# A four-layer kernel on one core: a twelfth paged sequence, staggered attention tiles, layer input added by VectorE, a later gate, and a new written order

## The chip, the cores and the metric

The kernel runs on one core of a Trainium2 chip. Its engines are PE (TensorE, matrix products), DVE (VectorE), ACT (ScalarE), POOL (GpSimd, here mostly the issuer of indirect DMAs) and SP (which issues the plain DMAs). Each engine takes its instructions in the order of the program; semaphores hold an instruction back until what it needs is there. The metric is the device time of one execution in microseconds (us), as the median of several runs.

## The reference, cut to what matters

The input is 8 sequences of 512 tokens with 128 features. Four layers follow, each added to its input, which is normalised first:

```
x = x + attention(layernorm(x))      # one head, causal, softmax
x = x + ffn(layernorm(x))            # 32 experts, 4 per token, and a shared expert
x = x + rwkv(layernorm(x))           # time mixing with a scan over the tokens, then channel mixing
x = x + ffn(layernorm(x))            # the same weights again
```

The expert layer, `swiglu(x, w1, w2, w3) = silu(x @ w1) * (x @ w3) @ w2`:

```
scores = softmax(x @ Wg); weights, indices = top_k(scores, 4)
for e in range(32):
    tok = tokens that chose e, the first C = 2048 of them
    y[tok] += swiglu(x[tok], W1[e], W2[e], W3[e]) * weight
y += swiglu(x, Ws1, Ws3, Ws2)        # the shared expert, for every token
```

W1 and W3 are 128 x 64 per expert, W2 is 64 x 128. Everything is in float32.

## The kernel before, in words

**Where things lie.** The 8 sequences stay on the chip in `res[b]` (128 tokens x 4 blocks x 128 features) through all four layers; all weights are loaded once. Matrix products write into PSUM tiles: `light` gives one of four single banks, and `ps2` has two tiles of two banks for the wide results.

**Streams.** The work is cut into streams, Python generators that are advanced one step at a time: `a0` to `a7` (`attention`, which ends in the routing `route` of the first expert layer), `r0` to `r7` (`rwkv`, ending in the routing of the second expert layer), and for the two expert layers (first letter small or other for the first, the next for the second) `x`/`y` (`shared`), `s`/`t` (`scatter`), `u`/`v` (`combine`), `d`/`D` (`full_up`), `e`/`E` (`full_down`) and the four stages of a group of experts `k l m n`/`K L M N` (`turned`, `up`, `down`, `give`, L558 to L617). The string `ORDER` (L82), two letters a step, is the order written out by hand in which these steps are issued; `play` walks it. Since all engines keep the program's order, this string decides what stands ahead of what on every engine, the DMA queues of SP and POOL included.

**The expert layers, two ways.** `RUNS` (L35) says for each of the two expert layers which sequences are done how.

- *Full* (`full_up`, `full_down`): every token of the sequence goes through all 32 experts, two at a time (16 pairs). PE makes two products of 128 x 512 per pair (L706), ACT the tanh (L709), DVE three passes (L712 to L714), the last two with the gates, which come back from DRAM by broadcasting loads (L695). `full_down` sums all pairs in one PSUM tile: it starts with the identity times the layer's input (L722), then adds four products per pair (`down_on`, L676), and ACT copies the sum into `res` (L727).
- *Paged*: `route` gives every (token, choice) a row in a buffer in DRAM in which rows of one expert fill whole pages of 128. `scatter` (L505) writes the normalised rows there: 16 indirect DMAs per sequence from POOL, a short memset after each (`pause`, L307). A group of sequences shares the pages: a group of three has 80 pages, a group of two 64, taken in units of four. Per unit, `turned` loads the pages and transposes them (L345, copy L563), `up` multiplies by the expert's weights (L575), DVE computes the gate's exponent (L580), ACT the tanh and the exponential (L583, L584), and DVE makes the gated product (L586, L587) and multiplies it by the gate (L588, L589). `down` transposes it (L596, copies L601), and `give` multiplies by the second weights (L608), copies the result (L614) and stores it in DRAM on SP's queue. `combine` (L656) then adds the results into `res`: 16 indirect DMAs with addition per sequence from POOL. The first of them needs all units of the group.

In the first expert layer, sequences 1 to 3 and 4 to 6 are paged groups and 0 and 7 are full; in the second, 0 to 2 and 4 to 5 are groups and 3, 6 and 7 are full: 11 paged, 5 full. Sequences of the second layer use the same two DRAM buffers again. Group (f, g) below is group g of expert layer f, both counted from 0.

**The shared expert** (`shared`, L519): two products with the normalised input, tanh and two DVE passes between, then the identity times the layer's input (L537) and four products with Ws2 into one PSUM tile, which ACT copies into `res` (L540).

**Attention** (`attention`, L732): after the norm and the three projections, four query tiles of 128 are done one after the other, each in seven steps: scores (L762), mask and row maximum, the maximum times minus the scale (L767), exponential with row sum (L771), transposes (L775) and a copy, product with V (L782), and the sum into `res` (L787).

## Time and profile before

| | |
|---|---|
| median of three runs | 837.41 us (836.06 to 840.99) |
| the profiled execution | 835.56 us, span 833.9 us |
| granted TensorE clock, mean | 0.977 |
| PE busy | 766.4 us (92%) |
| DVE busy | 607.6 us (73%) |
| POOL busy | 569.7 us (68%) |
| ACT busy | 472.0 us (57%) |
| indirect DMAs issued by POOL | 176 scatters, 176 gathers |

The span runs from the first to the last instruction of one profiled execution. Busy time is the union of an engine's instructions; what an engine spends on issuing a DMA's descriptors counts, the short gap before each issue does not. The page gives the span in 40 slices of 20.8 us, a digit per slice in tenths of busy time, and the granted TensorE clock in the same way. Groups of instructions are given by line: engine, operation, what is written and read, the count, the busy time, the mean length of one in ns, and the engine's idle time just before them with what ended it. A table by stage has for each stretch its length and then PE's, the weight loads', DVE's, ACT's and POOL's busy time with the number of instructions, the granted clock, the DMA engines' share and GB/s. In lists of waits a line has the waiting instruction, what released it, and the total us, times and longest us.

### The profile page before, as it was taken

The page shows a single profiled execution, that of the slowest core. Times are in us where ns is not written, and L with a number is a line of the kernel's source. Part 1 is how long each engine was busy: PE and PEld are TensorE (multiplying, and loading weights), DVE is VectorE, ACT ScalarE, POOL GpSimd, SP SyncE. Part 2 cuts the span into 40 slices and gives each one's busy share as a digit, 9 for nine tenths or more (in the row PEclk, how much of TensorE's full clock was granted, in tenths as well). Part 3 has the DMA queues.
Part 4 walks back from the last instruction along what each step waited for, and adds up shares of the span by engine and source line. Part 5 has one row for each costly group of instructions (what it writes and reads, how often), then busy time and mean ns, then how long its engine had stood idle before and what let it go on. Part 6 is the DMA issues. An engine that isn't in the chain of part 4 may idle for free.

```text
span 833.9 us, 14386 instructions
## 1 busy us (share of the span) xinstructions
PE 766.4 (92%) x4206; PEld 536.3 (64%) x4206; DVE 607.6 (73%) x2017; ACT 472.0 (57%) x1124; POOL 569.7 (68%) x634
## 2 busy tenths in 40 slices
PE   3998989899999999897998899999999999999993
PEld 2666667577876686684544555555878986776562
DVE  4677877778777558898867778978898664576672
ACT  3875633445776766673747267354677876542221
POOL 6312888742881887888888888885037057888876
PEclk9999999999999999999999789999999999999997
DMA  9999513533749767455222225253246679777663
GB/s 280 262 200 257 143 44 96 141 90 87 196 127 236 134 137 145 131 111 125 30 29 29 35 27 126 65 131 89 65 116 179 167 175 226 150 149 148 135 124 55
DMA packets 154460, 108.19 MB, mean 130 GB/s; under 512 B 17648, under 2 KB 140912, under 8 KB 154128
## 3 DMA queue, kind: packets, MB, share of 16 engines
q1 hardware_dynamic: 122976, 82.74, 41.0%
q0 software_dynamic: 30976, 23.27, 16.1%
q10 hardware_dynamic: 432, 1.27, 0.5%
q8 instruction: 36, 0.59, 0.3%
q14 instruction: 40, 0.33, 0.2%
HBM read 62.40 MB, written 44.84 MB: 129 GB/s over the span
## 4 chain that ended last, share of the span: by engine, by line
PE 35%; POOL 28%; issue 15%; DVE 10%; DMA 6%; ACT 4%; POOLq 1%; SPq 0%; DVEq 0%; ACTq 0%
POOL res L656 18%; POOL xs L505 6%; PE acl L575 5%; PE ac L706 4%; PE o L608 4%; PE turn_x L345 2%; DMA res<-ys,rows 2%; PE fsum L676 2%; POOL idle L307 2%; PE kv L938 2%; PE kk L929 2%; PE o L782 1%; PE acl L596 1%; PE lg L373 1%; DMA res<-in_x_dram 1%
## 5 line engine op out<-in xcount | busy, mean ns | idle before, releaser
L656 POOL DMA_INDIRECT res<-ys,rows x176 | 282.1, 1603 | 82.7 <-issue 48.4
L505 POOL DMA_INDIRECT xs<-xn,rows x176 | 182.1, 1034 | 79.0 <-issue 27.5
L706 PE MATMUL ac<-fT,pair 128*128 128x512 f32 x320 | 152.1, 599 | 0.0
L709 ACT ACTIVATE fh<-ac 128x512 f32<-128x512 f32 x80 | 47.7, 597 | 101.5 <-PE ac L706 101.0
L676 PEld LDWEIGHTS fsum<-w2s,fh 128*128 128x128 f32 x640 | 79.5, 193 | 23.7 <-DVE fh L714 10.9
L676 PE MATMUL fsum<-w2s,fh 128*128 128x128 f32 x640 | 84.1, 277 | 3.5 <-DVE fh L714 2.8
L706 PEld LDWEIGHTS ac<-fT,pair 128*128 128x128 f32 x320 | 56.5, 193 | 47.4 <-issue 45.9
L575 PE MATMUL acl<-w13s,xgTs 128*128 x608 | 83.0, 280 | 2.2 <-ACT hz L601 0.8
L575 PEld LDWEIGHTS acl<-w13s,xgTs 128*128 128x128 f32 x608 | 75.6, 193 | 13.4 <-issue 5.3
L712 DVE SCALAR_TENSOR_TENSOR fh<-fh,ac 128x512 f32<-128x512 f32 x80 | 54.4, 680 | 40.4 <-ACT fh L709 40.0
L608 PE MATMUL o<-w2s,hz 128*128 x608 | 79.3, 276 | 1.5 <-ACT gT L492 1.3
L608 PEld LDWEIGHTS o<-w2s,hz 128*128 128x128 f32 x608 | 73.9, 192 | 5.6 <-issue 2.6
L601 ACT COPY hz<-acl 64x256 f32<-64x256 f32 x152 | 55.6, 366 | 16.5 <-PE acl L596 14.5
L583 ACT ACTIVATE h<-acl 128x256 f32<-128x256 f32 x76 | 29.1, 382 | 53.6 <-DVE wt L580 50.3
L714 DVE TENSOR_TENSOR fh<-fh,g 128x512 f32<-128x512 f32 x80 | 55.4, 693 | 2.8
L713 DVE TENSOR_TENSOR g<-g,ac 128x512 f32<-128x512 f32 x80 | 54.3, 679 | 0.0
L334 POOL TENSOR_TENSOR rstd_f<-rstd_f,nhalf 128x4 f32<-128x4 f32 x16 | 19.4, 1213 | 49.3 <-DVE wt L580 23.2
L586 DVE SCALAR_TENSOR_TENSOR h<-h,acl 128x256 f32<-128x256 f32 x76 | 31.7, 418 | 25.6 <-ACT h L583 25.4
L307 POOL MEMSET idle<- 128x192 f32 x176 | 49.2, 280 | 0.1
L563 ACT COPY xgTs<-turn_x 128x512 f32<-128x512 f32 x76 | 44.3, 584 | 6.7 <-PE turn_x L345 4.9
L614 ACT COPY oc<-o 128x512 f32<-128x512 f32 x76 | 44.2, 586 | 5.7 <-PE o L608 3.2
L345 PE MATMUL turn_x<-ident,xg 128*128 128x128 f32 x304 | 45.3, 273 | 2.1 <-DMA xg<-xs 2.0
(265 smaller groups left out, 1551.6 us busy)
## 6 DMA issues: line engine op xcount, KB each, us to landing
g<-gd SPq DMA_DIRECT2D x40, 512.0 KB, 6.9
xg<-xs SPq DMA_DIRECT2D x76, 260.0 KB, 3.7
ys<-oc SPq DMA_DIRECT2D x76, 256.0 KB, 2.5
xs<-zero SPq DMA_DIRECT2D x4, 2600.0 KB, 14.6
xs<-xn,rows POOLq DMA_INDIRECT x176
res<-ys,rows POOLq DMA_INDIRECT x176
res<-in_x_dram SPq DMA_DIRECT2D x8, 256.0 KB, 4.5
pair<-in_w_dram SPq DMA_DIRECT2D x1, 2048.0 KB
```

What stands on the lines that cost most here:

```text
L307: nc.gpsimd.memset(idle, 0.0)
L345: nc.tensor.transpose(p[:, j * P : (j + 1) * P], src[:, j, :P], ident)
L505: i = nc.gpsimd.indirect_dma_start(out=xs[g][:, :], out_offset=bass.IndirectOffsetOnAxis(ap=rows[:, j, k : k + 1], axis=0), in_=xn[:, j, : ...
L575: nc.tensor.matmul(acl[:, j, :EW], xT[:, j * P : (j + 1) * P], w13f[:, bass.ds(at[j], EW)], start=True, stop=True)
L601: nc.scalar.copy(z[half, i, :].rearrange("p (j c) -> p j c", c=H), hT[half])
L608: nc.tensor.matmul(o[:, j * P : (j + 1) * P], z[:, j % 2, j // 2 * P : (j // 2 + 1) * P], w2h[j % 2][:, bass.ds(at[j], P)], start=True, st ...
L656: nc.gpsimd.indirect_dma_start(out=xa[:, j, :], out_offset=None, in_=ys[g][:, :], in_offset=bass.IndirectOffsetOnAxis(ap=rows[:, j, k : k ...
L676: nc.tensor.matmul(p[:, j * P : (j + 1) * P], h[:, j * P : (j + 1) * P], w, start=False, stop=stop and j == NJ - 1)
L706: nc.tensor.matmul(ac[:, s, :], pair[:, i, s, :], xT, start=True, stop=True)
L712: nc.vector.scalar_tensor_tensor(h, h, 1.0, ac[:, 0, :], ALU.add, ALU.mult)
L713: nc.vector.tensor_tensor(v, v, ac[:, 1, :], ALU.mult)
L714: nc.vector.tensor_tensor(h, h, v, ALU.mult)
```

## The change

- `RUNS`: sequence 3 of the second expert layer is paged instead of full, in a group with 4 and 5. Both groups of that layer have 80 pages now; 12 sequences are paged, 4 full.
- `shared`: the identity product is gone. A paged sequence's four products go into PSUM alone, and DVE adds them to `res`. For a full sequence the stream ends before the product with Ws2; `full_down` begins its sum with that product, has no identity product either, and DVE adds the sum to `res`.
- `LATE_GATES`: in group (0, 0) and group (1, 1) the gate is no longer multiplied in ahead of the second weights by DVE (L589); ACT multiplies it in while it copies the result out of PSUM, in four activations with a scale per row instead of one copy. The gate tiles get six buffers instead of four.
- Attention: minus the scale goes into the copy of the queries, the mask is +1e30 and the row minimum is taken, and L767 falls away. The four query tiles become generators of seven steps that are started three steps apart.
- `ORDER` is another string: 2249 steps instead of 2276.

The diff, with the string left out:

```diff
--- before.py
+++ after.py
@@ -34,12 +34,16 @@
 PAGED, FULL = True, False
 RUNS = (
     ((FULL, 0, 1), (PAGED, 1, 4), (PAGED, 4, 7), (FULL, 7, 8),),
-    ((PAGED, 0, 3), (FULL, 3, 4), (PAGED, 4, 6), (FULL, 6, 8),),
+    ((PAGED, 0, 3), (PAGED, 3, 6), (FULL, 6, 8),),
 )
 PAGES = [[(lo, hi) for kind, lo, hi in runs if kind] for runs in RUNS]
 G = max(len(p) for p in PAGES)
 GB = max(hi - lo for p in PAGES for lo, hi in p)
 UNIT = 4
+
+
+
+LATE_GATES = ((0, 0), (1, 1))
 
 
 def pages_of(n):
@@ -80,54 +84,53 @@
 
 
 ORDER = (
...
 )
 
 
@@ -225,7 +228,7 @@
     ident = const.tile([P, P], F32, tag="ident", name="ident")
     make_identity(nc, ident)
     cmask = const.tile([P, P], F32, tag="cmask", name="cmask")
-    make_causal_mask(nc, cmask, mask_val=-1e30)
+    make_causal_mask(nc, cmask, mask_val=1e30)
     ones = const.tile([P, P], F32, tag="ones", name="ones")
     nc.gpsimd.memset(ones, 1.0)
     tri = const.tile([P, P], F32, tag="tri", name="tri")
@@ -532,12 +535,15 @@
         nc.tensor.matmul(p3, W("Ws3"), xT, start=True, stop=True)
         yield
         nc.vector.scalar_tensor_tensor(h, h, 0.5, p3, ALU.mult, ALU.mult)
+        if run_of(f, b)[0] is FULL:
+            hidden[f, b] = h
+            yield
+            return
         yield
         p = light(f"s2_{n}")
-        nc.tensor.matmul(p, ident, flat(xa), start=True, stop=False)
-        down_on(p, h, W("Ws2"), True)
-        yield
-        nc.scalar.copy(flat(xa), p)
+        down_on(p, h, W("Ws2"), start=True, stop=True)
+        yield
+        nc.vector.tensor_tensor(flat(xa), flat(xa), p, ALU.add)
         yield
 
     def experts(f, g):
@@ -546,6 +552,7 @@
         nb = PAGES[f][g][1] - PAGES[f][g][0]
         nu = pages_of(nb) // UNIT
         loaded, first, mid, last = {}, {}, {}, {}
+        late_gate = (f, g) in LATE_GATES
 
         def load(u):
             if u < nu:
@@ -576,7 +583,7 @@
                     acl[:, j, :EW], xT[:, j * P : (j + 1) * P], w13f[:, bass.ds(at[j], EW)], start=True, stop=True
                 )
             yield
-            wt = st.tile([P, UNIT], F32, tag="wt", name=f"wt_{n}_{u}")
+            wt = st.tile([P, UNIT], F32, tag="wt", name=f"wt_{n}_{u}", bufs=6)
             nc.vector.tensor_tensor(wt, acl[:, :, P], xg[:, :, P], ALU.add)
             yield
             h = mo.tile([P, UNIT, H], F32, tag="h", name=f"h_{n}_{u}")
@@ -586,11 +593,12 @@
             nc.vector.scalar_tensor_tensor(h, h, 1.0, acl[:, :, :H], ALU.add, ALU.mult)
             nc.vector.tensor_tensor(h, h, acl[:, :, H:P], ALU.mult)
             nc.vector.tensor_tensor(wt, wt, xg[:, :, P + 1], ALU.mult)
-            nc.vector.tensor_tensor(h, h, wt.unsqueeze(2).to_broadcast([P, UNIT, H]), ALU.mult)
-            mid[u] = (at, h, acl[:, :, EW + 1 : EW + 1 + H])
+            if not late_gate:
+                nc.vector.tensor_tensor(h, h, wt.unsqueeze(2).to_broadcast([P, UNIT, H]), ALU.mult)
+            mid[u] = (at, h, wt, acl[:, :, EW + 1 : EW + 1 + H])
 
         def down(u):
-            at, h, hT = mid.pop(u)
+            at, h, wt, hT = mid.pop(u)
             pairs = flat(h)
             for i in range(UNIT // 2):
                 nc.tensor.transpose(hT[:, 2 * i : 2 * i + 2, :], pairs[:, i * P : (i + 1) * P], ident)
@@ -599,10 +607,10 @@
             for i in range(2):
                 half = slice(i * H, (i + 1) * H)
                 nc.scalar.copy(z[half, i, :].rearrange("p (j c) -> p j c", c=H), hT[half])
-            last[u] = (at, z)
+            last[u] = (at, z, wt)
 
         def give(u):
-            at, z = last.pop(u)
+            at, z, wt = last.pop(u)
             o = light(f"o_{n}_{u}")
             for j in range(UNIT):
                 nc.tensor.matmul(
@@ -611,7 +619,11 @@
                 )
             yield
             oc = mo.tile([P, UNIT, P], F32, tag="oc", name=f"oc_{n}_{u}")
-            nc.scalar.copy(flat(oc), o)
+            if late_gate:
+                for j in range(UNIT):
+                    nc.scalar.activation(oc[:, j, :], o[:, j * P : (j + 1) * P], AF.Copy, scale=wt[:, j : j + 1])
+            else:
+                nc.scalar.copy(flat(oc), o)
             nc.sync.dma_start(
                 out=ys[g][u * UNIT * P : (u + 1) * UNIT * P].rearrange("(j p) d -> p j d", p=P), in_=oc
             )
@@ -670,14 +682,14 @@
     def store(b):
         nc.sync.dma_start(out=out[b].rearrange("(j p) d -> p j d", p=P), in_=res[b])
 
-    def down_on(p, h, w, stop=False):
+    def down_on(p, h, w, start=False, stop=False):
 
         for j in range(NJ):
             nc.tensor.matmul(
-                p[:, j * P : (j + 1) * P], h[:, j * P : (j + 1) * P], w, start=False, stop=stop and j == NJ - 1
+                p[:, j * P : (j + 1) * P], h[:, j * P : (j + 1) * P], w, start=start and j == 0, stop=stop and j == NJ - 1
             )
 
-    ready = {}
+    ready, hidden = {}, {}
 
     def full_up(f, b):
 
@@ -719,14 +731,46 @@
 
         xa = res[b]
         p = light(f"fsum_{f}_{b}")
-        nc.tensor.matmul(p, ident, flat(xa), start=True, stop=False)
+        down_on(p, hidden.pop((f, b)), W("Ws2"), start=True)
         yield
         for i in range(NP):
-            down_on(p, ready.pop((f, b, i)), w2s[:, 1 + 2 * i, :P], i == NP - 1)
-            yield
-        nc.scalar.copy(flat(xa), p)
+            down_on(p, ready.pop((f, b, i)), w2s[:, 1 + 2 * i, :P], stop=i == NP - 1)
+            yield
+        nc.vector.tensor_tensor(flat(xa), flat(xa), p, ALU.add)
         if f == 1:
             store(b)
+        yield
+
+    def attend(b, i, qT, kT, vs, scale):
+
+        xa = res[b]
+        n = (i + 1) * P
+        s = light(f"s_{b}_{i}")
+        nc.tensor.matmul(s[:, :n], qT[:, i * P : n], kT[:, :n], start=True, stop=True)
+        yield
+        nc.vector.tensor_tensor(s[:, i * P : n], s[:, i * P : n], cmask, ALU.add)
+        big = st.tile([P, 1], F32, tag="abig", name=f"abig_{b}_{i}")
+        nc.vector.tensor_reduce(big, s[:, :n], AX.X, ALU.min)
+        yield
+        pr = block([P, S], name=f"pr_{b}_{i}")
+        den = st.tile([P, 1], F32, tag="aden", name=f"aden_{b}_{i}", bufs=8)
+        nc.scalar.activation(pr[:, :n], s[:, :n], AF.Exp, bias=big, scale=-1.0, accum_out=den)
+        yield
+        p = light(f"prT_{b}_{i}")
+        for j in range(i + 1):
+            nc.tensor.transpose(p[:, j * P : (j + 1) * P], pr[:, j * P : (j + 1) * P], ident)
+        yield
+        prT = block([P, S], name=f"prTs_{b}_{i}")
+        nc.scalar.copy(prT[:, :n], p[:, :n])
+        yield
+        o = light(f"o_{b}_{i}")
+        for j in range(i + 1):
+            nc.tensor.matmul(
+                o[:, :P], prT[:, j * P : (j + 1) * P], vs[:, j * P : (j + 1) * P], start=(j == 0), stop=(j == i)
+            )
+        yield
+        nc.vector.reciprocal(den, den)
+        nc.vector.scalar_tensor_tensor(xa[:, i, :], o[:, :P], den, xa[:, i, :], ALU.mult, ALU.add)
         yield
 
     def attention(b):
@@ -745,7 +789,7 @@
             nc.tensor.matmul(p, W(w), xT, start=True, stop=True)
             yield
             t = block([P, S], name=f"{w}T_{b}")
-            nc.scalar.copy(t, p)
+            nc.scalar.activation(t, p, AF.Copy, scale=-scale if w == "WQ" else 1.0)
             qk.append(t)
             yield
         qT, kT = qk
@@ -756,36 +800,13 @@
         vs = block([P, S], name=f"vs_{b}")
         nc.scalar.copy(vs, p)
         yield
-        for i in range(NJ):
-            n = (i + 1) * P
-            s = light(f"s_{b}_{i}")
-            nc.tensor.matmul(s[:, :n], qT[:, i * P : n], kT[:, :n], start=True, stop=True)
-            yield
-            nc.vector.tensor_tensor(s[:, i * P : n], s[:, i * P : n], cmask, ALU.add)
-            big = st.tile([P, 1], F32, tag="abig", name=f"abig_{b}_{i}")
-            nc.vector.tensor_reduce(big, s[:, :n], AX.X, ALU.max)
-            nc.vector.tensor_scalar(big, big, -scale, None, ALU.mult)
-            yield
-            pr = block([P, S], name=f"pr_{b}_{i}")
-            den = st.tile([P, 1], F32, tag="aden", name=f"aden_{b}_{i}")
-            nc.scalar.activation(pr[:, :n], s[:, :n], AF.Exp, bias=big, scale=scale, accum_out=den)
-            yield
-            p = light(f"prT_{b}_{i}")
-            for j in range(i + 1):
-                nc.tensor.transpose(p[:, j * P : (j + 1) * P], pr[:, j * P : (j + 1) * P], ident)
-            yield
-            prT = block([P, S], name=f"prTs_{b}_{i}")
-            nc.scalar.copy(prT[:, :n], p[:, :n])
-            yield
-            o = light(f"o_{b}_{i}")
-            for j in range(i + 1):
-                nc.tensor.matmul(
-                    o[:, :P], prT[:, j * P : (j + 1) * P], vs[:, j * P : (j + 1) * P], start=(j == 0), stop=(j == i)
-                )
-            yield
-            nc.vector.reciprocal(den, den)
-            nc.vector.scalar_tensor_tensor(xa[:, i, :], o[:, :P], den, xa[:, i, :], ALU.mult, ALU.add)
-            yield
+
+        tiles = [attend(b, i, qT, kT, vs, scale) for i in range(NJ)]
+        for t in range(7 + 3 * (NJ - 1)):
+            for i in range(NJ):
+                if 0 <= t - 3 * i < 7:
+                    next(tiles[i])
+                    yield
         if b + 1 < G:
             clear(b + 1)
         yield from route(xa, 0, b)
```

## The prediction

> **What bounds the kernel now.** I read the busy shares first, then the span in slices, the table by stage, the waits of POOL by stage, and last the costliest groups for prices.
>
> ```profile
> span 833.9 us, 14386 instructions
> ...
> PE 766.4 (92%) x4206; PEld 536.3 (64%) x4206; DVE 607.6 (73%) x2017; ACT 472.0 (57%) x1124; POOL 569.7 (68%) x634
> ...
> PE   3998989899999999897998899999999999999993
> ...
> POOL 6312888742881887888888888885037057888876
> PEclk9999999999999999999999789999999999999997
> ```
>
> ```profile
> 250.00:575.00 325.00, 301.11 (x1421) 191.52 (x1419) 253.83 (x767) 192.76 (x431) 267.11 (x244) 0.97 0.49 101
> 575.00:675.00 100.00, 99.25 (x696) 81.96 (x695) 78.54 (x268) 69.80 (x178) 26.49 (x37) 1.00 0.46 123
> 675.00:834.00 159.00, 143.63 (x794) 100.56 (x794) 91.39 (x202) 64.61 (x146) 125.26 (x81) 0.97 0.74 144
> ```
>
> ```profile
> L656 POOL DMA_INDIRECT res<-ys,rows x176 | 282.1, 1603 | 82.7 <-issue 48.4
> L505 POOL DMA_INDIRECT xs<-xn,rows x176 | 182.1, 1034 | 79.0 <-issue 27.5
> L706 PE MATMUL ac<-fT,pair 128*128 128x512 f32 x320 | 152.1, 599 | 0.0
> ...
> L676 PE MATMUL fsum<-w2s,fh 128*128 128x128 f32 x640 | 84.1, 277 | 3.5 <-DVE fh L714 2.8
> ```
>
> ```profile
> POOL xs L505 <- DVE h L587: 27.2, 1, 27.2
> POOL res L656 <- DMA ys<-oc: 24.4, 1, 24.4
> ```
>
> Two engines take turns. PE is busy in 99.25 of the 100 us from 575 to 675 while POOL (fifth number of the stage rows) works 26.5: there PE sets the time, and the two long waits of POOL in the last fence (for sequence 5's rows, then for the last expert results of the second layer's first group) lie in this stage. From 250 to 575 and from 675 on POOL is the full engine: a gather repeats every 1.60 + 0.27 = 1.88 us (the issue gap of 48.4 us over 176 is not counted busy), a scatter with its pause every (182.1 + 49.2 + 27.5)/176 = 1.47 us, so 267 busy us of 325 are nearly all of it. In the tail 80 gathers run from 673.6 to 828.8 us, 1.94 us each, and the span ends 5.2 us later.
>
> **The change part by part.** The profiled execution took 835.6 us, 1.7 us over its span; the median of the runs, 837.4, is 1.9 above it. I sum against the span and add 1.7.
>
> *Sequence 3 of the second layer goes from full to paged.* PE loses a fifth of L706 (30.4 us), of fsum L676 (16.8) and of the gate transposes L489 (0.6). It gains four units of four pages (80 + 80 + 80 + 64 pages become four times 80): per unit L345 45.3/76, L575 83.0/76, L596 29.6/76, L608 79.3/76, together 3.12, so 12.5 us. POOL gains 16 scatters and 16 gathers: 16 x (1.47 + 1.88) = 53.6 us. DVE: 16 x (0.69 + 0.68 + 0.68) = 32.8 us less, 4 x 1.58 more for the units. ACT: 16 x 0.60 less, 4 x 2.48 more. SP: eight gate loads of 512 KB and a 64 KB store less, four loads and four stores of about 256 KB more; the DMA engines are 58% taken (41.0 + 16.1 + 0.5 in the queue rows), so I price it at nothing; the cover is the two units of lead that page loads have, and without it a unit waits one landing, 3.7 us.
>
> *The identity matmuls L537 and L722 go* (16.5 + 5.1 us of PE; one of the five L722 belonged to sequence 3 and is in this sum). In their place DVE adds once for each of 12 paged and 4 full sequences, 128x512 with a PSUM operand: 0.68 us as L534, 10.9 us in all; 16 + 5 copies of 0.58 leave ACT. A full sequence's shared product now goes straight into the open sum.
>
> *Attention.* The negating L767 goes (4.9 us of DVE); the sign rides in a copy that is made anyway. The staggering moves work only inside a sequence. In the attention rows PE idles 4.8 us ahead of L775, 1.4 ahead of L782 and 0.6 ahead of L762; it can win these 6.8 us or lose as much again, since each engine still takes its steps in the written order. I take nothing.
>
> *The late gate,* 40 units. DVE loses L589, 40 x 0.426 = 17.0 us. ACT's one copy of 0.586 us becomes four 128x128 activations with a scale per row. No row has that form: below lies the plain 128x128 copy of L778 at 0.267 us, above L326 (scale and bias per row) at 26.3/64 = 0.41, so 4 x 0.267 - 0.586 = 0.48 to 4 x 0.41 - 0.586 = 1.06 us a unit, 19 to 42 us. I take 0.30 each, nearer the copy, since only one operand is read per row: +25 us. ACT ends near 490 us of busy time and bounds nothing over the span. While group (0,0)'s results are made, ACT's row sums (scaled by 472/518, as for PE below) come to 62 us beside PE's 69, and to 70 by the upper price: the cover is then gone, and the stretch 20 x 0.39 = 8 us longer.
> [...]
>
> **Sums by engine.** The groups' busy times add to 894 us on PE, the union is 766: pipelined matmuls overlap, so I scale row sums by 0.857. PE: -30.4 - 16.8 - 0.6 + 12.5 - 16.5 - 5.1 = -56.9, times 0.857 = -48.8, leaving 717.6. POOL: the total of occupied time goes from 652 to 705. DVE loses some 36 us. So PE's work shrinks by 49 us and POOL's grows by 54: the result hangs on whether POOL's present idle time can be filled.
>
> **Walking the order.** Each token of the written order is one step; I add the row prices of its instructions to its engine. For the present order this gives at each point how much work PE (scaled) and POOL have been handed, and the trace says when it was there:
> - First scatter: PE 62.1, in the trace 77.3 (15.2 later).
> - First gather (sequence 2, needs all of group (0,0)): last expert product at PE 234.4, in the trace 268.8 (34.4 later, of which about 2 are POOL's own wait for a norm, L334).
> - First gather to last scatter of sequence 4: POOL 300.0, in the trace 305.8, a factor 1.019: no idle time beyond the sums.
> - Last product of the second layer's first group: PE 618.7, gather in the trace 673.6 (54.9 later).
>
> The same walk for the new order:
> - First scatter: PE 70.1 + 15.2 = 85 us. The scatters of group (0,0) hold 70 us of POOL and end at 155 (150.6 before), and the first page is readable some 8.5 us later as before, 164, where PE arrives at 158: about 5 us of new PE stall; the next late thing is the group's results.
> - Last product of (0,0): PE 219.3, so the first gather at 219.3 + 34.4 - 2 + 4 = 256 us, 13 earlier.
> - From there to sequence 5's last scatter and one norm POOL holds 350.6 x 1.019 = 357 us: 613. Are the data there? Sequence 5 of the second layer ends at PE 508 + 54 + 8 = 570 us, POOL reaches its scatters at 588: yes, by 18. The last product of the second layer's first group is at PE 537.3 + 54.9 = 592: yes, by 21. Both long waits of the last fence are then gone, and POOL is what is late.
> - 96 gathers at 1.94 = 186: 799. Halfway, at 706, they need the second group's results, which PE ends at 629.2 + 54.9 = 684.
> - Plus 5.2 to the end: span 804, plus 1.7: **806 us**. PE ends at 717.6 + 55 + 4 = 777, so some 27 us of what it gains turn into waiting for POOL.
>
> Moved steps that stand in a queue ahead of others: sequence 5's scatters are in POOL's queue ahead of all 96 gathers, so each us beyond the 18 moves the end by one. On SP the stores of finished sequences wait for their last gathers with page loads behind them: sequence 1's store comes at PE 597 + 55 = 652, POOL ends that sequence at 613 + 55 x 1.03 = 670; 4 more to land; PE has two loaded units (6 us), so it stalls some 16 us, inside the 22 of slack at 706. The shared adds of the second layer all stand ahead of the gathers into the same rows, so no gather waits for them.
>
> **The rivals.**
> - *PE sets the end.* If POOL's gaps close better (gathers at 1.88, no stall at the first page): 252 + 351 + 180 + 5 = 788, or with PE alone 717.6 + 55 = 773 span, 775 to 790 us. For it: PE is full in most slices today. Against: POOL alone needs 350.6 + 180 us after about 250. Chance 0.13.
> - *The chain of a sequence is longer than the order supposes.* Today 124 us lie between sequence 5's last gather (494 by the sums) and its first scatter (618.3). POOL's last gather for it comes at 474 now; with 124 us its scatters start at 598, not 588: 816; with one or two more such joints (SP's stores, the ACT stretch at +8) 820 to 833. Chance 0.13.
> - *Slower: PE is held back in the stage that POOL paces.* The granted clock was 0.86 and 0.80 from 450 to 500 us, where PE was idle longest (6.1 us in 25). With POOL the pace for all of 256 to 613, such a clock could hold throughout. At 0.80 over these 357 us PE is 71 us later, less some 11 that the 0.97 there already costs. Against sequence 5's margin of 18 this leaves 42 us: 806 + 42 = 848. It decides from 36 us beyond the margin, a mean clock near 0.82. Against: the clock is 1.00 in most slices even of the POOL stage. Chance 0.09 for slower, 0.05 for landing within 0.5% of 837.4.
> [...]
> - *The change does not do what it says:* a fifth of L706 staying is not possible with the full run cut from the table; no chance given.
>
> **How the numbers follow.** The main case has the rest, 0.60, with its own range of 794 to 820 (first gather at 250 to 264, ACT's bounds 8 us wide, gathers at 1.88 to 1.97). The range for 8 in 10: from 782, below which lies half of the PE case (0.06), to 832, above which lie the slower case and the near one (0.14). A measurement of this kernel can tell about 0.5% from no change: under 833.2 is faster: 0.60 + 0.13 + 0.13 = 0.86; 0.05 within; 0.09 slower.
>
> **What would show it.** Right: L706 at x256 and about 122 us; L656 and L505 at x192; no L537 or fsum<-res; POOL over 80% busy in every slice from about 256 us to the end with no single wait over 10 us; PE's busy time near 718, its idle time near 85; first gather near 256, the tail's first near 613. Wrong: a POOL wait of tens of us ahead of sequence 5's scatters or of the second layer's first gather, a granted clock under 0.9 for long, or a first gather after 275.

## The result and the profile after

The changed kernel takes 812.99 us (median of four runs, 810.9 to 814.69); the kernel before took 838.33 beside it. The ratio is 0.9696, with an interval of 0.9657 to 0.9734. The forecast was 806. In a later set of runs the ratio was 0.969 [0.9658, 0.9721]. The profiled execution took 812.43 us over a span of 810.7. Some runs on one chip, of the kernels below with the gate early and with all three undone, were in a slower state; times are medians of the fast runs.

The head of the page of the changed kernel, then its span in 40 slices of 20.3 us (a digit is the busy share in tenths):

```profile
span 810.7 us, 14263 instructions
...
PE 719.2 (89%) x4056; PEld 514.6 (63%) x4056; DVE 575.5 (71%) x1952; ACT 480.8 (59%) x1230; POOL 616.6 (76%) x682
...
PE   3999899989979989999889986989889999999993
...
POOL 5312888378876888888888888889865888878776
PEclk9999999999998999999989999799999999999997
```

The table by stage of the changed kernel (bounds and length, then busy us of PE, weight loads, DVE, ACT, POOL; granted clock, DMA share, GB/s):

```profile
250.00:575.00 325.00, 288.70 (x1464) 193.09 (x1463) 251.11 (x841) 199.99 (x457) 280.30 (x269) 0.96 0.46 97
575.00:675.00 100.00, 90.69 (x641) 74.84 (x639) 61.41 (x204) 75.35 (x211) 75.96 (x72) 1.00 0.65 152
675.00:811.00 136.00, 119.09 (x609) 79.04 (x607) 80.23 (x164) 47.14 (x118) 105.09 (x67) 0.96 0.69 135
```

POOL is the pace from its first gather at 246.9 us to the last at 803.7, but for one place below; the runs with more and with less work for POOL bear that out. From 575 to 675 it now works 76 us where it worked 26.5, and PE, which filled those 100 us, has 9 left over. PE's busy time fell by 47 us, the span by 23: the other half became waiting of PE. The groups of the changed kernel that carry the prices:

```profile
L668 POOL DMA_INDIRECT res<-ys,rows x192 | 308.4, 1606 | 75.6 <-issue 54.2
L508 POOL DMA_INDIRECT xs<-xn,rows x192 | 197.2, 1027 | 54.4 <-issue 29.0
L718 PE MATMUL ac<-fT,pair 128*128 128x512 f32 x256 | 120.9, 600 | 1.3 <-DVE g L725 1.3
L688 PE MATMUL fsum<-w2s,fh 128*128 128x128 f32 x512 | 71.6, 288 | 7.7 <-DVE fh L726 7.1
```

One place is not as forecast. The two long waits of POOL (27.2 and 24.4 us) are not there any more, but between sequence 5's last scatter and the second layer's first gather POOL stands still twice. Its timeline in the changed kernel (start, duration, instruction; in brackets the idle time ahead of it and what ended that):

```profile
579.11 0.97 POOL L508 DMA_INDIRECT xs<-xn,rows  x1 [0.17 <-ACT wt L591]
...
601.57 0.97 POOL L508 DMA_INDIRECT xs<-xn,rows  x1 [0.16 <-issue]
602.54 0.27 POOL L310 MEMSET idle<- 128x192 f32 x1
608.94 1.41 POOL L337 TENSOR_TENSOR rstd_c<-rstd_c,nhalf 128x4 f32<-128x4 f32 x1 [6.13 <-DVE rstd_c L335]
616.37 1.63 POOL L668 DMA_INDIRECT res<-ys,rows  x1 [6.02 <-DMA xg<-xs]
```

I call the stretch from 602.8 to 616.4 the joint: 12.2 us of waiting and 1.4 of a norm. The line at 579.11 is sequence 5's first of 16 scatters: no wait ahead of it, though the 18 us that POOL was to be late there are gone too.

### The profile page after: what moved, and what is told of

It reads as the page before. It is cut to its first block, busy times and chain, and to the rows that moved or that the text cites. A ratio compares the mean times of both kernels' runs of the same rounds, so it can differ in the third digit from the quotient of the medians.

```text
span 810.7 us, 14263 instructions
## 1 busy us (share of the span) xinstructions
PE 719.2 (89%) x4056; PEld 514.6 (63%) x4056; DVE 575.5 (71%) x1952; ACT 480.8 (59%) x1230; POOL 616.6 (76%) x682
## 3 DMA queue, kind: packets, MB, share of 16 engines
q10 hardware_dynamic: 432, 1.27, 0.5%
## 4 chain that ended last, share of the span: by engine, by line
POOL 34%; PE 23%; issue 19%; DVE 11%; DMA 7%; ACT 3%; POOLq 1%; SPq 0%; DVEq 0%; ACTq 0%
POOL res L668 22%; POOL xs L508 8%; PE ac L718 3%; PE acl L582 3%; PE o L616 3%; POOL idle L310 2%; DMA res<-ys,rows 2%; PE fsum L688 1%; PE s L749 1%; DMA xg<-xs 1%; DMA gd<-gT 1%; PE o L768 1%; DVE wden L909 1%; DMA res<-in_x_dram 1%; PE turn_x L348 1%
## 5 line engine op out<-in xcount | busy, mean ns | idle before, releaser
L668 POOL DMA_INDIRECT res<-ys,rows x192 | 308.4, 1606 | 75.6 <-issue 54.2
L508 POOL DMA_INDIRECT xs<-xn,rows x192 | 197.2, 1027 | 54.4 <-issue 29.0
L718 PE MATMUL ac<-fT,pair 128*128 128x512 f32 x256 | 120.9, 600 | 1.3 <-DVE g L725 1.3
L721 ACT ACTIVATE fh<-ac 128x512 f32<-128x512 f32 x64 | 38.1, 596 | 103.0 <-PE ac L718 98.8
L688 PEld LDWEIGHTS fsum<-w2s,fh 128*128 128x128 f32 x512 | 66.5, 200 | 26.0 <-DVE fh L726 16.7
L688 PE MATMUL fsum<-w2s,fh 128*128 128x128 f32 x512 | 71.6, 288 | 7.7 <-DVE fh L726 7.1
L718 PEld LDWEIGHTS ac<-fT,pair 128*128 128x128 f32 x256 | 45.7, 194 | 40.9 <-issue 36.8
L624 ACT ACTIVATE oc<-o,wt 128x128 f32<-128x128 f32 x160 | 45.3, 377 | 6.8 <-PE o L616 4.7
L348 PEld LDWEIGHTS turn_x<-ident,xg 128*128 128x128 f32 x320 | 38.0, 144 | 17.3 <-issue 12.1
L726 DVE TENSOR_TENSOR fh<-fh,g 128x512 f32<-128x512 f32 x64 | 44.4, 694 | 2.2
L725 DVE TENSOR_TENSOR g<-g,ac 128x512 f32<-128x512 f32 x64 | 43.5, 680 | 2.7 <-DMA g<-gd 2.7
```

What stands on the lines that cost most here:

```text
L348: nc.tensor.transpose(p[:, j * P : (j + 1) * P], src[:, j, :P], ident)
L508: i = nc.gpsimd.indirect_dma_start(out=xs[g][:, :], out_offset=bass.IndirectOffsetOnAxis(ap=rows[:, j, k : k + 1], axis=0), in_=xn[:, j, : ...
L624: nc.scalar.activation(oc[:, j, :], o[:, j * P : (j + 1) * P], AF.Copy, scale=wt[:, j : j + 1])
L668: nc.gpsimd.indirect_dma_start(out=xa[:, j, :], out_offset=None, in_=ys[g][:, :], in_offset=bass.IndirectOffsetOnAxis(ap=rows[:, j, k : k ...
L688: nc.tensor.matmul(p[:, j * P : (j + 1) * P], h[:, j * P : (j + 1) * P], w, start=start and j == 0, stop=stop and j == NJ - 1)
L718: nc.tensor.matmul(ac[:, s, :], pair[:, i, s, :], xT, start=True, stop=True)
```

## The experiments

Each was timed against the kernel before on the same chip, and the edits are to the changed kernel unless said otherwise. In brackets stand the ratio to the kernel before and its interval. The theory on record: POOL's work sets the end, PE's relief is worth only what lets POOL start earlier, and identity products, gate and staggering are worth little. The rivals: PE still sets much of the time; or the chain of a sequence does.

**What POOL's time is worth.** The pause behind each scatter is doubled, or left out.

```
 def pause():
     nc.gpsimd.memset(idle, 0.0)
+    nc.gpsimd.memset(idle, 0.0)      # pause twice, in either kernel
---
-    nc.gpsimd.memset(idle, 0.0)      # no pause
+    return
```

> The kernel after, with the memset behind each of the 192 scatters issued twice: POOL holds some 0.29 us more per scatter. Theory (POOL paces from the first gather at 247 us to the end, but for a joint of 12 us at 603 to 616 us where it waits for PE): 96 scatters lie in that stretch, 96 x 0.29 = 28 us; the joint can take up to 12 of them, the 48 scatters ahead of the first page can add up to 14. So 829 to 853 us, I take 840. Rival (PE at 89% still sets the time, POOL only follows): at most 6 us, 812 to 819.

> The kernel after without the memset behind each scatter: POOL holds 0.28 us less per scatter, 27 us less in the stretch that POOL paces. Theory: POOL gives way to the next late thing, PE, whose own sums put the last product of the second layer's first group at 592 instead of 612 us: 8 to 20 us faster, 793 to 805. Rival (PE sets the time): within 4 us of 813. A third possibility is that the pauses keep scatters from crowding the DMA queue; then the scatters themselves become longer than 1.03 us and the time does not fall.

> The kernel before with the memset twice. 64 scatters lie between its first gather and 574 us (18.6 us more for POOL), 16 more in the gap in which POOL waited 27 us. Theory (in the kernel before PE sets the time from 575 to 675 us, and POOL's waits of 27 and 24 us there take up the delay): 0 to 9 us slower than the kernel before. Rival (POOL sets its time throughout): 18 us slower or more.

Measured: 926.05 us with two pauses (1.1051 of the kernel before [1.0986, 1.1116]) and 798.5 with none (0.9515 [0.9444, 0.9585]), so +113 and -14.5 against the 812.99 of the first set (the kernel before took 838.91 here and 838.33 there). The kernel before with two pauses took 926.57 (1.1064 [1.0998, 1.113]), +88: I had thought that it would absorb nearly all of it, and that the changed kernel would lose some 27. A part of both misses is a wrong price. Groups of the changed kernel with two pauses, then with none:

```profile
L509 POOL DMA_INDIRECT xs<-xn,rows x192 | 195.6, 1019 | 112.1 <-issue 80.5
...
L311 POOL MEMSET idle<- 128x192 f32 x192 | 50.2, 262 | 11.0
```

```profile
L508 POOL DMA_INDIRECT xs<-xn,rows x192 | 196.9, 1025 | 88.9 <-issue 48.5
```

The issue gap ahead of a scatter is 0.30 us behind another scatter, 0.17 behind one pause and 0.47 behind two, so a scatter repeats every 1.27, 1.41 and 2.03 us. The second pause costs 0.62 us, 119 over 192 scatters; taking the first away wins only 0.14, 27. Against these prices 113 of 119 reached the end, 14.5 of 27, and in the kernel before 88 of 176 x 0.62 = 109. So the end follows POOL in both kernels, in the changed one almost us for us when POOL is made slower and by half when it is made faster. Where the time comes in is seen from POOL's first gather: in the kernel before, and there with two pauses; then in the changed kernel, there with two pauses and with none:

```profile
268.84 1.64 POOL L656 DMA_INDIRECT res<-ys,rows  x1 [0.83 <-DMA xg<-xs]
309.03 1.64 POOL L657 DMA_INDIRECT res<-ys,rows  x1 [0.52 <-DMA xg<-xs]
246.85 1.64 POOL L668 DMA_INDIRECT res<-ys,rows  x1 [7.45 <-DMA xg<-xs]
305.47 1.64 POOL L669 DMA_INDIRECT res<-ys,rows  x1 [7.26 <-DMA xg<-xs]
244.47 1.64 POOL L668 DMA_INDIRECT res<-ys,rows  x1 [8.20 <-DMA xg<-xs]
```

In the changed kernel 96 scatters stand ahead of it. A second pause behind each costs 59.5 us by the price, and the first gather comes 58.6 later: more than half of the 113. Another 47 come up to sequence 5's first scatter (80 scatters) and 9 in its 16 scatters. Leaving the pause out saves 13 us of POOL ahead of the first gather, but only 2.4 reach it: the rest ends there in longer waits of POOL. My expectation rested on the scatters behind the first gather; to those ahead of it it gave 14 us at most. In the kernel before 40 of the 88 us come ahead of the first gather. So that POOL hardly mattered before, since PE filled 575 to 675, is refuted: with two pauses POOL's two long waits in the kernel before are still 27.3 and 27.1 us, so nothing was absorbed there. One thing moves along: the mean granted clock is 0.91 with two pauses (0.93 in the kernel before), 0.97 without. How much of the added time is a slower PE was not separated, but the scatters' price alone accounts for nearly all of it in the changed kernel.

The time with no pause lies in the expected range, but not for the expected reason: the last product ahead of the joint was to come at 592 us; it ends at 600.7, and the joint stays.

**What PE's time is worth.** The identity products and their copies are put back, or taken out of the kernel before.

```
+        nc.tensor.matmul(p, ident, flat(xa), start=True, stop=False)
-        down_on(p, h, W("Ws2"), start=True, stop=True)
+        down_on(p, h, W("Ws2"), stop=True)
-        nc.vector.tensor_tensor(flat(xa), flat(xa), p, ALU.add)
+        nc.scalar.copy(flat(xa), p)
```

> The kernel after with the identity products for the layer input back on PE, 16 of them (12 in the shared stream, 4 at the start of the full sums), and ACT's copies instead of DVE's additions: PE gets 16 x 1.03 x 0.857 = 14 us of work. Theory (POOL paces, PE only at the joint at 603 to 616 us): some ten of the products lie ahead of the joint, part of them in PE's waits: 3 to 9 us slower, 816 to 822. Rival (PE sets the time): all 14 us, 827. If POOL alone paced: 0.

> The kernel before with DVE adding the layer input, 21 identity products gone (18 us less for PE, by the rows), its order otherwise kept. Theory (PE sets the time of the kernel before from 575 to 675 us, and ahead of the first gather): the products in these stages count, 6 to 13 us faster, 825 to 832. Rival (its POOL or its chain of sequences sets the time throughout): within 3 us of the kernel before.

Put back, 811.54 us (0.9687 [0.9633, 0.9741]). The head of that kernel's page:

```profile
PE 732.4 (90%) x4088; PEld 518.4 (64%) x4088; DVE 567.6 (70%) x1936; ACT 489.1 (60%) x1246; POOL 616.1 (76%) x682
```

PE works 13 us more than in the changed kernel, DVE 8 less and ACT 8 more, and the end does not move, so in the new order the removal is worth nothing, less even than the few us I expected. Taken out of the kernel before (whose order also loses the ten steps that its full sequences then no longer have), on another chip, it made 888.65 us, 1.0119 [1.0072, 1.0166] of the kernel before, where I had expected a gain of 6 to 13. So work moved from PE to DVE is no gain in either kernel; why the kernel before lost 1% on that chip is open.

**Staggering and gate, first try.** The staggered loop becomes tile after tile; the late gate is taken away by an empty table; and a third kernel undoes both and the identity products, which leaves the paging and the order.

```
-        for t in range(7 + 3 * (NJ - 1)):
-            for i in range(NJ):
-                if 0 <= t - 3 * i < 7:
-                    next(tiles[i])
-                    yield
+        for i in range(NJ):
+            for t in range(7):
+                next(tiles[i])
+                yield
---
-LATE_GATES = ((0, 0), (1, 1))
+LATE_GATES = ()
```

> The kernel after with no late gates: in the two groups DVE multiplies the gate in ahead of the second weights again (40 x 0.426 = 17 us more on DVE, 40 x 0.55 = 22 us less on ACT). Theory (POOL paces from 247 us on, so DVE and ACT matter only ahead of the first gather and at the joint at 603 to 616 us): within 4 us of the kernel after, 809 to 817. Rival (DVE's relief is what made the groups quick): 5 to 12 us slower, 818 to 825.

> The kernel after with the four query tiles one after the other inside each attention, in the same written order of sequences. Theory: the chain of one tile then has fewer other steps between its own, so PE, ACT and DVE wait more in the first 150 us; the first scatter comes 3 to 12 us later than 77.7 us, and since POOL is full from the first gather on, this reaches the end: 814 to 825. Rival (the staggering is only a different order of the same work, hidden by the POOL waits of 8.6 and 7.3 us at 150 to 166 us): 811 to 814.

> The kernel after with identity products, early gates and unstaggered tiles: only the twelfth paged sequence and the new order are left of the change. Theory: these two carry the gain, the rest little: the sum of the three single steps, 812 to 828, still clearly under the kernel before. Rival (each part was needed): 828 or more.

Measured: 880.5 with the gate early (1.0021 [0.9986, 1.0056]), 909.08 unstaggered (1.0306 [1.025, 1.0362]), 910.2 with all three undone (1.0332 [1.0265, 1.04]). These three and the kernel before without identity products ran on a chip where the kernel before itself took 877 us, and the changed kernel was not timed there. So they are compared with one another alone. With a late gate in one and an early one in the other, the unstaggered kernel is 25 (by the ratios) to 29 us (by the medians) slower than the staggered: far more than the little expected, and the reason for the next pair. That paging and order alone would stay clearly under the kernel before did not come true: with all three undone the kernel is 3% over it on this chip.

**Staggering, with its pair on one chip.**

> The kernel after once more, as the measure for the others on the same chip: 813 us beside 838 for the kernel before, if the chip is like the first; on a chip like the last one (877 for the kernel before), 845 to 880.

> The kernel with unstaggered query tiles beside the kernel after on one chip. In its first run the first scatter came at 101 us instead of 77, and later points stayed late by about that. Theory: nothing behind it takes the delay up, so 18 to 28 us slower than the kernel after. Rival (the delay belonged to that chip): under 10 us.

Measured: 813.42 (0.969) and 837.67, which is 0.9985 [0.9964, 1.0006] of the kernel before. Staggering is worth 24 us in this order, about as much as the whole gain of 25.5. Without it nearly all of this is lost in the first 100 us. The stretch from 50 to 75 us of the unstaggered kernel, then of the changed one in its repeated run:

```profile
50.00:75.00 25.00, 16.94 (x81) 13.09 (x80) 8.59 (x35) 10.98 (x31) 1.01 (x1) 0.78 1.16 263
```

```profile
50.00:75.00 25.00, 23.94 (x159) 18.58 (x158) 18.31 (x103) 20.97 (x58) 3.02 (x3) 1.00 1.20 270
```

Waits of PE up to 110 us in the unstaggered kernel, then the one of the same kind in the changed one:

```profile
PE prT L761 <- ACT pr L757: 12.1, 9, 3.4
PE o L768 <- ACT prTs L764: 4.6, 5, 2.7
```

```profile
PE prT L761 <- ACT pr L757: 0.2, 1, 0.2
```

Unstaggered, one tile's chain of scores, exponential, transpose and product runs alone: PE waits for ACT 14 times, 16.7 us in all, its clock falls to 0.78, and it issues 81 products where the changed kernel issues 159. The first scatter comes at 98.8 us, not 77.1, and the delay stays to the end: first gather 274.5 against 250.1, last gather 830.2 against 806.4. This does not say that staggering is worth 24 us in any order: the new order was written for staggered tiles, and an order written for unstaggered ones with the new paging was not tried. Nor were staggered tiles in the kernel before. So it is shown that this order needs the staggering, but not how much the twelfth paged sequence gains by itself.

With this pair, the gate can be bounded loosely: unstaggered less staggered is 24 us with both gates late, and 25 to 29 on the other chip with the staggered one's gate early. So moving the gate is worth a few us at most, either way; that is an inference across two chips. On the other chip itself, gate and identity products undone together make the unstaggered kernel 1 to 2 us slower (1.0332 against 1.0306 of the kernel before, with overlapping intervals), which agrees.

**The joint.** One reading of the timeline was that the second group's first page, which waits for sequence 5's last scatter, stands ahead of the first group's last products in PE's written order and ahead of their stores in SP's. In the table of the order I moved the steps of the second groups (k to n in the first layer, the first of them by 13 places; K to N in the second, the first of them by 20; both by less and less further on) to later places. An excerpt, in which `K1` (page loads of the second group) comes behind the last `N0` (results of the first):

```
-"r7M0N0M0N0N0L0L0L0L0K0K0K0r7r7L0K0M0M0L0N0L0L0N0L0K0K0L0N0L0M0M0L1K1r7L1L0L0N0N0M0L0L0L0K1N0r6r7"
-"M0M0K1r6M0N0N0N0N0K1L1L1K1r6r7v0L1L1L1L1r6L1r7M1r7M1y2y4K1L1K1r6M1L1y1r6y2L1r6M1K1L1N1L1N1r6K1r6"
+"r7M0N0M0N0N0L0L0L0L0K0K0K0r7r7L0K0M0M0L0N0L0L0N0L0K0K0L0N0L0M0M0L1r7L0L0N0N0M0L0L0L0N0r6r7M0M0r6"
+"M0N0N0N0N0K1L1r6r7v0K1r6r7K1r7y2y4K1L1r6L1K1y1r6L1y2L1L1r6L1L1M1M1r6K1r6L1K1M1L1L1r6M1v2K1L1N1L1"
```

> The kernel after, where the second group's streams of page loads, transposes and products (in both expert layers) are moved some 14 and 24 steps later in the order, so that they stand behind the first group's last three result stores on SP's queue and its last two products on PE. Theory (at both joints SP waits for the scatters of the second group, 4.1 and 4.0 us, with the stores ahead of the first gather queued behind it, and POOL waits 7.4 and 12 us for those stores): the waits ahead of the first gather (246.9 us) and of the 97th (616.4 us) shrink to a few us, 5 to 14 us faster than the kernel after in this call. Rival (the first group's own products are late): within 3 us.

> As the run before, and without the memset behind the scatters. Theory: the two gains concern different us of POOL and add up, 14 us for the pauses as measured: 18 to 28 us faster than the kernel after. Rival (PE, at 713 us of work and full in the tail, becomes the end): no more than the 14 us of the pauses.

Measured: 824.2 us (0.9826 [0.9795, 0.9857]), 11 slower than the changed kernel where I had expected a gain, and without the pause 810.71 (0.9642 [0.9599, 0.9684]), 3 faster than the changed kernel where 18 to 28 were expected, and 12 slower than no pause alone on another chip. The joint lasts 12.2 us, 10.8 of them waits (13.6 and 12.2 in the changed kernel), and 14 us were lost in the first layer, between the first gather (242.8) and the last (482.5, 7 us later than in the repeated run of the changed kernel although it began 7 earlier): POOL works as long there as before (193.6 us in either), but waits 6.2, 5.7 and 3.0 us for three norms, where the changed kernel waits 0.9 us for one. So this reading is not enough. The landmarks of runs on chips where the kernel before takes 837 to 839 us, from each trace's POOL timeline and DVE's last write of sequence 5's rows, in us:

| kernel | first gather | first layer's last gather | sequence 5's rows ready | its first scatter | its last scatter | next gather | rows to next gather |
|---|---|---|---|---|---|---|---|
| before | 268.8 | 492.2 | 617.6 | 618.3 | 640.6 | 673.6 | 56.0 |
| changed | 246.9 | 473.1 | 577.9 | 579.1 | 601.6 | 616.4 | 38.5 |
| changed, repeated | 250.1 | 475.8 | 581.0 | 581.9 | 604.6 | 619.1 | 38.1 |
| no pause | 244.5 | 468.1 | 568.6 | 569.3 | 589.7 | 604.7 | 36.1 |
| loads later | 242.8 | 482.5 | 587.6 | 588.4 | 611.2 | 624.7 | 37.1 |
| loads later, no pause | 238.6 | 469.8 | 572.6 | 573.3 | 593.7 | 609.5 | 36.9 |
| unstaggered | 274.5 | 500.3 | 605.7 | 606.6 | 629.3 | 642.5 | 36.8 |
| pause twice | 305.5 | 538.5 | 675.3 | 685.0 | 716.8 | 731.2 | 55.9 |

Two chains can be seen. From the rows to the next gather 36 to 38.5 us pass whether the 16 scatters between take 21 us or 23: PE has that much written work before the first group's last products are stored, so POOL, done 22 to 25 us after the rows, waits for the rest. Without the pause this is seen best: PE waits only 0.4 us for the second group's page, it is busy 31.3 of the 34.4 us behind the rows, and the joint lasts as long. And with the second group's loads in the way, the last scatter sets it. PE's timeline with two pauses (722.30) and the waits of SP's queue there:

```profile
722.30 1.09 PE L349 MATMUL turn_x<-ident,xg 128*128 128x128 f32 x4 [18.88 <-DMA xg<-xs]
723.18 0.64 PE L605 MATMUL acl<-ident,h 128*128 128x128 f32 x2
723.61 3.62 PE L617 MATMUL o<-w2s,hz 128*128 x16
```

```profile
SPq L561 <- DMA xs<-xn,rows: 19.9, 1, 19.9
```

The first group's last products L617 are held 18.9 us behind the transposes of a page that waits for the last scatter. In the changed kernel both chains end nearly together, the second with a small wait of 3.05 us; with the loads moved this wait ahead of the last products is gone, and they still end as late. The same stretch of PE in the changed kernel, then with the loads later:

```profile
605.75 0.41 PE L604 MATMUL acl<-ident,h 128*128 128x128 f32 x2
609.21 0.63 PE L348 MATMUL turn_x<-ident,xg 128*128 128x128 f32 x4 [3.05 <-DMA xg<-xs]
609.67 0.38 PE L604 MATMUL acl<-ident,h 128*128 128x128 f32 x2
609.89 2.26 PE L616 MATMUL o<-w2s,hz 128*128 x16
```

```profile
617.39 1.06 PE L616 MATMUL o<-w2s,hz 128*128 x8
619.16 1.16 PE L616 MATMUL o<-w2s,hz 128*128 x8 [0.72 <-ACT oc L626]
624.78 1.09 PE L348 MATMUL turn_x<-ident,xg 128*128 128x128 f32 x4 [4.46 <-DMA xg<-xs]
```

With the loads later the page comes behind the products, as meant, but the last products still end at 620, 33 us behind the rows. The kernel that would test it is one whose order puts the first group's last products ahead of sequence 5's routing; it was not tried, so it is argued, not shown, that this would shorten the joint.

## Why the prediction was right, and where it was off

*Sums by engine: right.* PE 719.2 us of busy time against 717.6, POOL 616.6 + 54.2 + 29.0 = 700 of occupied time against 705 (summed from the same rows the kernel before has 646, not 652, so it is 54 more, as forecast), ACT 481 against some 490, DVE 32 us less against 36. The share of L706 that was to go went: x256, 120.9 us where I said about 122.

*Late gate: right in the row.* Its four activations a unit take 45.3/160 = 0.283 us each, where the forecast took 0.30:

```profile
L624 ACT ACTIVATE oc<-o,wt 128x128 f32<-128x128 f32 x160 | 45.3, 377 | 6.8 <-PE o L616 4.7
```

The upper price of 0.41 from L326 was too high. The 8 us by which that price was to lengthen the stretch do not follow either: 70 us of ACT beside 69 of PE are one us more.

*The walk, landmark by landmark.*

| step | forecast | measured | its part in the end |
|---|---|---|---|
| first scatter | 85 | 77.7 | |
| group (0,0)'s scatters end | 155 | 147.0 | |
| first gather | 256 | 246.9 | -9 |
| POOL from there through sequence 5's scatters and one norm | 357 | 357, waits ahead of the norm left out | 0 |
| wait at the joint | none | 12.2 | +12 |
| 96 gathers | 186 | 189 | +3 |
| rest of the span | 5.2 | 5.3 | 0 |

So 804 - 9 + 12 + 3 = 810, the span measured. That PE's long waits of POOL could be filled with POOL's added work, and that POOL then sets the end, was right. That the number came so near is in part luck: two errors of opposite sign, and a first error made of two more, as follows.

*First gather, 9 us early: the mis-sized term is the staggering, taken at nothing.* The walk gave PE the lag of the old order up to the first scatter, 15.2 us; it was 7.6 with staggered tiles and 28.7 without them (98.8 - 70.1). So the new order by itself would have cost 13.5 us here, and staggering won 21; both were put at nothing. The bounds of 6.8 us came from PE's waits in the attention rows of the kernel before, whose order was another. Sums of work cannot see how often an order makes an engine wait for one tile's chain; and without staggering the forecast of faster would have been wrong, since that kernel takes as long as the kernel before. Nor does PE's work with a fixed lag set the first gather, as the walk had it: with two pauses, and no more work for PE, it came 58.6 us later.

*The joint: the step that failed is "Both long waits of the last fence are then gone, and POOL is what is late".* POOL came to sequence 5's scatters at 579, not 588, and the rows for them were ready at 577.9, not 570: of the 18 us of slack 1.2 were left. The first group's last products, put at 592, end at 612. The 54.9 us that the walk added there had been measured to the gather itself, store and landing included; to the gather it is now 79 (616.4 - 537.3). The working did not fit together here: it put sequence 5's rows 54 + 8 = 62 us behind PE's sums (it does not say what the 8 are), and the gather, which comes 29 us of PE's work later and also needs a store and a landing, only 54.9. With 62 it would have been 599, and the slack of 21 a mere 14. Measured, the rows are 70 us behind PE's sums, and the end of the last product 75: PE idles 36 us of the 325 from 250 to 575, where it idled 24 before.

*The long chain, a rival at 0.13: right in its place, too large in its size.* It had sequence 5's rows 124 us behind the last gather, as in the kernel before, and so 598. They came after 104.8. In the kernel before PE was full in that stretch (121.7 of 125.4 us); in the changed one it is busy 87.6 of the 104.8, and POOL, with 64 scatters and some norms, fills nearly all of it (93.5 us busy, and the issue gaps of 0.17 us ahead of its scatters are not counted). Without the pause it lasted 100.5, POOL then waiting 4.6 ahead of sequence 5: so a part of that saving is lost to this chain, and the larger part, 11 us, ahead of the first gather.

*Identity products:* the 16 that were put back, 13 us of PE's busy time, had bought nothing. The forecast had said that part of PE's gain would become waiting; it did not say which part.

*PE held back by its clock, the slower rival: not seen in its size.* The mean was 0.96 from 250 to 575, where by the forecast's own estimate it decides from about 0.82. What it is, finer slices of the changed kernel show (PE's busy time, count and clock):

```profile
502.00:504.00 2.00, 0.69 (x6) 1.00 0.14 48
504.00:506.00 2.00, 0.46 (x5) 0.84 0.06 19
506.00:508.00 2.00, 1.18 (x5) 0.50 0.10 33
...
512.00:514.00 2.00, 2.00 (x10) 0.50 0.12 37
514.00:516.00 2.00, 1.82 (x10) 0.60 0.10 33
516.00:518.00 2.00, 1.31 (x3) 1.00 0.20 67
```

The 0.80 that the slice from 500 to 525 us shows is a clock of one half for some 10 us. PE has two waits there, of 2.7 and 2.4 us with 1.2 us of work between, and none longer; in slices of 0.25 us the clock is still 1.00 from 505.0 to 505.25, within the second wait, and 0.50 from 505.5 to 505.75. So in this stretch a halved clock came with waits of under 3 us; what brings it down, and what brings it back, is not shown.

*SP's store of sequence 1 and the first page: neither stall came.* PE's waits for pages are 8.2 us in the whole run: 4.7 ahead of the first layer's second group, just before the first gather, 3.1 at the joint, and nothing of the 5 at the first page or the 16 behind that store. The first of these is the joint's second chain in the first layer: POOL waits 7.4 us ahead of its first gather there, and with the loads later that gather came 7 us earlier than in the repeated run, the one gain of that kernel.

*What would show it.* Right: L706's count, x192, no L537, PE's sum, no single wait of POOL over 10 us once its gathers run. Wrong: its slices are at 0.6 and 0.5 at the joint, and some slices of the tail show 7, because the issue gap of 0.30 us a gather is not counted busy. PE's idle time is 91.5, not 85.

## What to carry to other kernels

When two engines take turns, value each edit by the landmark that it moves, not by its busy time: 13 us of PE's work put back cost nothing here, and an edit without any work in it, the interleaving of four chains, was worth 24 in this order. In a walk of an order PE's lag at one point can be no smaller than at the point before it, since idle time only adds up; where forecast margins are of the size of the lags' errors, expect a wait at the joint. And look for the cheapest time to save on the engine that sets the pace: the changed kernel without the pause, 798.5 us, beats both kernels.

## What the runs showed of the hardware that was not expected

- A memset of 0.28 us between two scatters of POOL hides part of the issue gap (0.30 us without it, 0.17 with it), so that it costs only 0.14 net; a second one costs 0.62, since the gap grows to 0.47.
- The kernel before took 837 to 839 us in all sets of runs but one, and 877 us in that one, on a chip of its own. On that chip the changed kernel with an early gate took 0.2% more than the kernel before did there, with an interval that includes no change. The traces there have single stalls of 5 to 18 us between 100 and 300 us for which no other instruction is named as the cause. Whether the whole change gains on that chip was not measured and stays open.
